# A three-layer max-aggregation graph network: blocks of two kinds interleaved, byte stores moved to ScalarE's queue, and the cut of long edge lists changed

## The chip, the cores and the metric

One core of one Trainium2 chip runs the whole kernel. The metric is the device time of one execution in microseconds; the time before is the median of 3 runs. TensorE (PE) multiplies, VectorE (DVE) takes maxima, ScalarE (ACT) builds one-hot matrices, GpSimd (POOL) issues indirect gathers, SyncE (SP) issues nearly all other transfers from one in-order queue.

## The reference

```python
N, E, D, H = 6250, 200000, 128, 256          # nodes, edges (sorted by dst), widths
h = relu(layernorm(x))
for Wl, bl, Wr in three layers (128->256, 256->256, 256->128):
    agg = segment_max(h[src], dst, N)        # 0 where a node has no edge
    h = leaky_relu(agg @ Wl + bl + h @ Wr, 0.01)
out = x + h
```

`dst` is drawn as 6250 u², so the first nodes have hundreds of edges and the last some ten.

## The kernel before

**Tiles and blocks.** The nodes are cut into 50 tiles of 127. Two neighbouring tiles of sources form a group `g`, 25 in all, taken from 24 down to 0. For every group and every tile of destinations, the kernel holds per destination node at most one source in the group (or two, one for each tile `s` of the pair). A one-hot matrix (`hot`) times the two tiles of features (`pair_sb`) puts that source's features into PSUM (`pg`, three buffers), and DVE takes the maximum with the running result `acc`. Features are split in two parts so that the products are exact, hence two products for each output.

**Units.** A destination tile is *narrow* (one source for a pair: both `s` add up in one `pg`, one maximum for a step) or *wide* (one source for each `s`: two `pg` and two maxima for a step, with the same products). There are four sets, numbered `k`: 0 is 24 narrow tiles, 1 is 8 *virtual* units (1024 rows of at most 64 edges that stand for the 381 nodes with the most edges; each is a wide unit and a narrow one called `x`), 2 is 19 wide tiles, 3 is 4 narrow tiles. A block `(layer, k, g)` is cut into steps of 8 products: in the layers 1 and 2 (the second and third) a block has 6, 4, 5 and 1 steps for k = 0 to 3, so that a layer has 400 steps; layer 0, with half the width, has 225.

**Edges that don't fit.** Edges left over (a second source in the same group) stand in lists, one list for each set, sorted by length: `CAPS[k][q]` is how many entries the q-th column of 128 rows may have. Each entry is one indirect gather of 128 feature rows on POOL (`g`, L997, with a small `pace_t` memset behind it); DVE folds them (L1012, L1017), and SP stores the result to `best` (L1021). If some list is longer than its cap, a slow general path computes everything anew.

**Nodes.** When a set's products and lists are done, `Node` runs for each of its tiles: gather from `best` (L1041), transposes, maximum `mz`, the two linear products (L1070, L1072), and for layers 0 and 1 the stores that feed the next layer (`table`, `across`, `pair`). For the virtual set, `Joined` first merges and scans the 1024 rows and sends them to `joined`; then the three tiles with the longest lists have their nodes.

**What sets the order.** One loop over steps writes all engines' programs. It takes the steps in the order of `steps`: within a layer, all blocks of k = 0, then 1, 2, 3. Lists, nodes and setup work are planned at step numbers (`agenda`), counted from `ends_at[layer, k]`, the step at which a set's blocks end: 150, 250, 375 and 400 of a layer's 400 before. `load_pair` runs two blocks ahead (three buffers), `load_idx` three ahead.

**One-hots.** In layer 0, `one_hot` reads the stored source numbers (`idx_sb`), writes `away` (bytes, three buffers; L924) and from it `hot` (six buffers; L931). `away` is also stored to `far` in DRAM (450 stores, L926), so that the layers 1 and 2 can make `hot` from it directly. SP's queue carries these stores, each one issued when the next one-hot is made (`unsent`). ACT must wait for a store to land before it writes that `away` buffer again.

Of the kernel before, what the change touches and what calls it, by code (L numbers as in the profile page):

```python
# [32 lines left out]
F32 = mybir.dt.float32  # L33
# [6 lines left out]
OP = mybir.AluOpType  # L40
AX = mybir.AxisListType

P = 128
# [6 lines left out]
CUT = 64  # L50
# [3 lines left out]
VT, NV = 3, 8  # L54
CAPS = (
# [4 lines left out]
)  # L60
# [8 lines left out]
def kernel(ctx: ExitStack, tc: tile.TileContext, x, src, dst,  # L69
                    Wl1, bl1, Wr1, Wl2, bl2, Wr2, Wl3, bl3, Wr3, out):  # L70
    nc = tc.nc
# [5 lines left out]
    NG = NT // 2  # L77
# [15 lines left out]
    GROUPS = (  # L93
        [("n", i) for i in range(24)],
        [("w", NW + v) for v in range(NV)],
        [("w", i) for i in range(NW)],
        [("n", i) for i in range(24, NN)],
    )
# [20 lines left out]
    psum = ctx.enter_context(tc.tile_pool(name="psum", bufs=1, space=bass.MemoryType.PSUM))  # L119
# [28 lines left out]
    far = [dram.tile([P, NG, DW[k]], U8, name=f"far{k}") for k in range(len(GROUPS))]  # L148
# [12 lines left out]
    first = setup.enter_context(tc.tile_pool(name="first", bufs=1))  # L161
# [181 lines left out]
    at_n = edge.tile([P, NT], F32, name="at_n")  # L343
    at_i = edge.tile([P, NT], I32, name="at_i")
    count_n = edge.tile([P, NT], F32, name="count_n")
# [30 lines left out]
    rem = edge.tile([P, NV], F32, name="rem")  # L376
# [261 lines left out]
    def virtual():  # L638

        nrow_i = first.tile([P, VT], I32, name="nrow_i")  # L640
        nc.vector.tensor_scalar(nrow_i, count_n[:, :VT], float(CUT - 1), None, op0=OP.add)
        nc.vector.tensor_scalar(nrow_i, nrow_i, CUT.bit_length() - 1, None, op0=OP.arith_shift_right)
        nrow = first.tile([P, VT], F32, name="nrow")
        nc.vector.tensor_copy(nrow, nrow_i)
        pre = first.tile([P, VT], F32, name="pre")
        nc.vector.memset(pre, 0.0)
        for c in range(1, VT):
            nc.vector.tensor_add(pre[:, c : c + 1], pre[:, c - 1 : c], nrow[:, c - 1 : c])
        v_p = psum.tile([P, VT], F32, tag="z", name="v_p")
        nc.tensor.matmul(v_p, before, nrow, start=True, stop=False)  # L650
        nc.tensor.matmul(v_p, ones, pre, start=False, stop=True)
        iota_r = first.tile([P, NV * P], F32, tag="xs0", name="iota_r")
        for v in range(NV):
            nc.vector.tensor_scalar(iota_r[:, v * P : (v + 1) * P], iota_f, float(v * P), None, op0=OP.add)
        vs = first.tile([P, VT], F32, name="vs")
        nc.vector.tensor_copy(vs, v_p)
        ve = first.tile([P, VT], F32, name="ve")
        nc.vector.tensor_add(ve, vs, nrow)
        ab = first.tile([P, VT, 2], F32, name="ab")
        nc.vector.scalar_tensor_tensor(ab[:, :, 0], vs, -float(CUT), at_n[:, :VT], op0=OP.mult, op1=OP.add)  # L660
        nc.vector.scalar_tensor_tensor(ab[:, :, 1], vs, float(CUT), count_n[:, :VT], op0=OP.mult, op1=OP.add)
        of_p = psum.tile([P, NV, 2], F32, tag="tr", name="of_p")
        sels = []
        for c in range(VT):
            under = first.tile([P, NV * P], F32, tag="xs1", name="under")
            nc.vector.tensor_scalar(under, iota_r, ve[:, c : c + 1], None, op0=OP.is_lt)
            sel = first.tile([P, NV * P], F32, tag=f"xs{2 + c}", name="sel")
            nc.vector.scalar_tensor_tensor(sel, iota_r, vs[:, c : c + 1], under, op0=OP.is_ge, op1=OP.mult)
            sels.append(sel)
        for v in range(NV):  # L670
            for c in range(VT):
                nc.tensor.matmul(
                    of_p[:, v, :], sels[c][:, v * P : (v + 1) * P], ab[:, c, :], start=(c == 0), stop=(c == VT - 1)
                )
        has = first.tile([P, VT], F32, name="has_v")
        nc.vector.tensor_scalar(has, nrow, 1.0, None, op0=OP.min)
        starts = first.tile([P, VT, NV * P], BF16, tag="pr0", name="starts", bufs=2)
        for c in range(VT):
            nc.vector.tensor_scalar(
                starts[:, c, :], iota_r, vs[:, c : c + 1], has[:, c : c + 1], op0=OP.is_equal, op1=OP.mult  # L680
            )
        st_p = psum.tile([P, 2, 512], F32, tag="pg", name="st_p", bufs=3)
        for h in range(2):
            for c in range(VT):
                nc.tensor.matmul(
                    st_p[:, h, :], ones_h, starts[:, c, h * 512 : (h + 1) * 512], start=(c == 0), stop=(c == VT - 1)
                )
        by_row = first.tile([P, NV], F32, name="by_row")
        nc.vector.tensor_scalar(by_row, iota_f[:, :NV], float(P), part_f, op0=OP.mult, op1=OP.add)
        nc.vector.tensor_scalar(by_row, by_row, float(CUT), None, op0=OP.mult)  # L690
        nc.vector.tensor_tensor(pos_i, of_p[:, :, 0], by_row, op=OP.add)
        nc.vector.tensor_tensor(rem, of_p[:, :, 1], by_row, op=OP.subtract)
        nc.vector.tensor_scalar(
            mask_v, st_p.rearrange("p h c -> p (h c)"), -2.0, 1.0, op0=OP.mult, op1=OP.add
        )
        nc.vector.tensor_scalar(mask_v, mask_v, BIG, None, op0=OP.mult)
        last = first.tile([P, VT], F32, name="last")
        nc.vector.scalar_tensor_tensor(last, ve, -float(NV * P + 1), has, op0=OP.add, op1=OP.mult)
        nc.vector.tensor_scalar(last, last, 0.0, float(NV * P), op0=OP.min, op1=OP.add)
        nc.vector.tensor_copy(last_i, last)  # L700
        beyond = first.tile([P, VT], F32, name="beyond")
        nc.vector.tensor_scalar(beyond, ve, float(NV * P), None, op0=OP.is_gt)
        nc.vector.reduce_sum(over[:, 4:5], beyond, axis=AX.X)
# [168 lines left out]
    def chunks(layer, k):  # L872

        n = 8 if widths[layer] == P else 4
        units = PLANES[k]
        for w in "wnx":
            us = [i for i, u in enumerate(units) if u[0] == w]
            for i0 in range(0, len(us), n):
                part = us[i0 : i0 + n]
                yield part[0] - (NV if w == "x" else 0), len(part) * P, part[0], units[part[0]][1] if w == "w" else None  # L880
# [31 lines left out]
                yield us[i0], len(us[i0 : i0 + HOT // P]) * P, len(GROUPS[k]) if w == "w" else 0  # L912

    hots, live, done_with = {}, [0], [0, 0]
    unsent = []

    def one_hot(layer, k, g, c, w, odd, s):

        t, of = idx_q[layer, k, g]
        put = 2 * c * P + s * w  # L920
        if layer == 0:
            at = of + (c + (odd if s else 0) + (NV if PLANES[k][c] in EXTRA else 0)) * P
            away = work.tile([P, HOT], U8, tag="away", name="away", bufs=3)[:, :w]
            nc.scalar.activation(away, t[:, at : at + w], AF.Abs, bias=near[:, s : s + 1], scale=1.0)  # L924
            if unsent:
                nc.sync.dma_start(*unsent.pop())  # L926
            unsent.append((far[k][:, g, put : put + w], away))
        else:
            away = t[:, of + put : of + put + w]
        hot = work.tile([P, HOT], F32R, tag="hot", name="hot", bufs=HOTS)  # L930
        nc.scalar.activation(hot[:, :w], away, AF.Relu, bias=1.0, scale=-1.0)  # L931
        hots[layer, k, g, c, s] = hot
        live[0] += 1

# [200 lines left out]


    steps, begins, ends_at = [], [], {}
    for layer in range(3):
        begins.append(len(steps))
        for k in range(len(GROUPS)):  # L1140
            for g in range(NG - 1, -1, -1):
                steps += [(layer, k, g, c) for c in chunks(layer, k)]
            ends_at[layer, k] = len(steps)
    begins.append(len(steps))
    agenda = {}
# [70 lines left out]
    for layer in range(3):  # L1216
# [45 lines left out]
        for k in range(NL):  # L1262
            t0 = max(ends_at[layer, k], done_at[k] + gap) + 1
# [22 lines left out]
            if k == NL - 1:  # L1286
                t0 = max(end, done_at[k] + 1) + 1
# [29 lines left out]
    def load_until(n):  # L1317
        while loaded[0] < min(n, len(blocks)):
            load_idx(*blocks[loaded[0]])
            loaded[0] += 1  # L1320

    def make_hots(t, most):

        while jobs_h and most and live[0] < HOTS and jobs_h[0][0] <= t + LOOK:
            most -= 1
            _, b, job = jobs_h.pop(0)
            if job[0] and unsent:
                nc.sync.dma_start(*unsent.pop())
            load_until(b + 1 + AHEAD)
            one_hot(*job)  # L1330

# [20 lines left out]
    for t in range(max(max(agenda)[0] + 1, len(steps) + 1)):  # L1352
# [10 lines left out]
        if t < len(steps):  # L1363
            st = steps[t]
            layer, k, g, _ = st
# [313 lines left out]
```

## Time and profile before

| | |
|---|---|
| Median of 3 runs | 3476.97 us (3474.94 to 3482.45) |
| The profiled execution | 3516.21 us, span 3514.4 us |
| PE busy | 2570.8 us (73%) |
| DVE busy | 2686.4 us (76%) |
| ACT busy | 1894.1 us (54%) |
| POOL busy | 2444.0 us (70%) |
| DMA | 639.71 MB, mean 182 GB/s |

No engine is busy throughout, and each stage has its own limit, so the shares of the whole span say little; the stages have to be read one by one. Counted along the products, setup ends at about 266 us, layer 0 runs to 1440, layer 1 to 2490, layer 2 to 3489.

### The profile page before, as it was taken

What the parts mean: (1) busy time and instruction counts of PE and PEld (TensorE: products, weight loads), DVE (VectorE), ACT (ScalarE), POOL (GpSimd) and SP (SyncE); (2) the same over time, 40 slices, a digit from 0 to 9 for tenths busy, and PEclk for the clock granted to TensorE, in tenths of its full rate; (3) what the DMA queues carried; (4) which work ended last, traced back from release to release, by engine and by line L of the source; (5) the groups of instructions that cost most, each with busy time, mean ns of one, the idle gap of its engine ahead of it and who ended that gap; (6) DMA issues with size and microseconds to landing.
All of it is one profiled execution on the core that took longest, in us unless ns stands there. A gap on an engine that the chain in (4) does not pass through costs nothing. (4 is left out here: it accounts for less than half of the span.)

```text
span 3514.4 us, 39180 instructions
## 1 busy us (share of the span) xinstructions
PE 2570.8 (73%) x9920; PEld 1816.2 (52%) x9920; DVE 2686.4 (76%) x4152; ACT 1894.1 (54%) x2762; POOL 2444.0 (70%) x3460
## 2 busy tenths in 40 slices
PE   1025642457766677799988978788999999787776
PEld 1013321234434444588766655556788776555555
DVE  6567799796555664588867989996688889899974
ACT  5106962687998997555434434343555534333432
POOL 5588742747667876388856867767388888777673
PEclk9976875579887777899999989999999999999998
DMA  9114421447866558676777755459776777655475
GB/s 293 44 42 124 142 87 42 110 121 212 232 177 187 181 168 244 214 211 217 215 219 225 211 163 169 158 162 306 255 214 226 225 222 204 177 173 168 147 221 172
DMA packets 347946, 639.71 MB, mean 182 GB/s; under 512 B 67830, under 2 KB 215939, under 8 KB 347073
## 3 DMA queue, kind: packets, MB, share of 16 engines
q1 hardware_dynamic: 268161, 438.67, 38.2%
q0 software_dynamic: 79488, 198.26, 22.5%
q8 instruction: 83, 1.36, 0.2%
q14 instruction: 150, 1.23, 0.1%
q10 hardware_dynamic: 64, 0.20, 0.0%
HBM read 494.73 MB, written 142.15 MB: 181 GB/s over the span
## 5 line engine op out<-in xcount | busy, mean ns | idle before, releaser
L948 PE MATMUL pg<-hot,pair_sb 128*128 128x512 f32 (+1 forms) x8000 | 2257.3, 429 | 536.5 <-ACT hot L931 249.6
L948 PEld LDWEIGHTS pg<-hot,pair_sb 128*128 128x128 f32 x8000 | 1540.3, 204 | 1124.2 <-ACT hot L931 442.3
L997 POOL DMA_INDIRECT g<-table,let x1530 | 1543.9, 1009 | 765.6 <-ACT let L986 320.7
L965 DVE TENSOR_TENSOR acc<-acc,pg 128x1024 f32<-128x1024 f32 (+3 forms) x1439 | 1647.2, 1168 | 484.1 <-PE pg L948 338.3
L931 ACT ACTIVATE hot<-idx_sb 128x1024 fp32r<-128x1024 uint8 (+2 forms) x900 | 827.0, 948 | 732.8 <-PE pg L948 463.1
L924 ACT ACTIVATE away<-idx_sb,near 128x1024 uint8<-128x1024 uint8 (+2 forms) x450 | 464.4, 1032 | 210.1 <-DMA far<-away 178.0
L1001 POOL MEMSET pace_t<- 128x300 bf16 x1530 | 560.3, 366 | 1.0
L931 ACT ACTIVATE hot<-away 128x1024 fp32r<-128x1024 uint8 (+2 forms) x450 | 427.7, 951 | 14.3
L1041 POOL DMA_INDIRECT agg<-best,end_i x141 | 138.6, 983 | 134.5 <-PE aT_p L1057 46.5
L1074 ACT COPY s<-z_p 127x256 f32<-127x256 f32 (+1 forms) x150 | 49.9, 333 | 329.4 <-PE z_p L1072 182.1
L1012 DVE TENSOR_TENSOR g<-g 128x1024 f32<-128x1024 f32 (+6 forms) x218 | 219.6, 1007 | 1.6 <-DMA g<-table,let 1.5
L1017 DVE TENSOR_TENSOR g<-g 128x512 f32<-128x512 f32 (+3 forms) x351 | 172.9, 493 | 10.2
L1070 PE MATMUL z_p<-wr,hT_in 128*128 128x256 f32 (+1 forms) x500 | 137.4, 392 | 7.1 <-DMA hT_in<-across 7.1
L1072 PE MATMUL z_p<-wl,mz 128*128 128x256 f32 (+1 forms) x500 | 122.0, 361 | 9.0 <-DVE mz L1063 7.6
L986 ACT ACTIVATE let<-ell 128x4 int32<-128x4 int16 (+3 forms) x444 | 81.5, 190 | 84.7 <-issue 84.7
L1063 DVE TENSOR_TENSOR mz<-acc,aT_p 128x256 f32<-128x256 f32 (+1 forms) x141 | 52.5, 372 | 83.5 <-PE aT_p L1057 62.0
L1072 PEld LDWEIGHTS z_p<-wl,mz 128*128 128x128 f32 x500 | 89.4, 204 | 21.7 <-DVE mz L1063 8.9
L1070 PEld LDWEIGHTS z_p<-wr,hT_in 128*128 128x128 f32 x500 | 80.0, 201 | 29.4 <-DMA hT_in<-across 7.6
L352 POOL DMA_INDIRECT win_d<-in_dst_dram,win_i x50 | 53.2, 1063 | 45.5 <-ACT rstd L305 14.7
L857 DVE TENSOR_TENSOR pr<-h,pr 128x256 fp32r<-128x256 f32 x100 | 42.4, 424 | 49.0 <-ACT pr L852 37.3
L622 POOL DMA_INDIRECT picks<-picked,to_i x55 | 57.2, 1039 | 30.0 <-DVE rank_f L599 14.1
L849 ACT COPY hT<-hT_p 128x254 f32<-128x254 f32 x100 | 36.3, 363 | 69.9 <-PE hT_p L847 61.1
(268 smaller groups left out, 1195.1 us busy)
## 6 DMA issues: line engine op xcount, KB each, us to landing
pair_sb<-pair SPq DMA_DIRECT2D x200, 512.0 KB
far<-away SPq DMA_DIRECT2D x350, 128.0 KB
idx_sb<-far SPq DMA_DIRECT2D x50, 768.0 KB
idx_sb<-far SPq DMA_DIRECT2D x50, 608.0 KB
pair_sb<-pair SPq DMA_DIRECT2D x100, 256.0 KB
pair<-pr SPq DMA_DIRECT2D x100, 256.0 KB
idx_sb<-far SPq DMA_DIRECT2D x50, 512.0 KB
g<-table,let POOLq DMA_INDIRECT x1530
```

Source lines behind the costliest of these rows:

```text
L924: nc.scalar.activation(away, t[:, at : at + w], AF.Abs, bias=near[:, s : s + 1], scale=1.0)
L931: nc.scalar.activation(hot[:, :w], away, AF.Relu, bias=1.0, scale=-1.0)
L948: nc.tensor.matmul(to, pr[:, s, i, kk * P : (kk + 1) * P], hot[:, o : o + bw], start=((alone or s == 0) and i == 0), stop=((alone or s == ...
L965: nc.vector.tensor_max(to, to, of)
L986: nc.scalar.activation(let[:, :n], ell[self.k][:, q, j : j + n], AF.Identity, scale=1.0)
L997: nc.gpsimd.indirect_dma_start(out=self.tiles[q, b][:, i, :], out_offset=None, in_=tables[self.layer], in_offset=bass.IndirectOffsetOnAxis ...
L1001: nc.gpsimd.memset(pace_t, 0.0)
L1012: nc.vector.tensor_max(base[:, : i + 1, :], base[:, : i + 1, :], g[:, : i + 1, :])
L1017: nc.vector.tensor_max(base[:, :h, :], base[:, :h, :], base[:, w - h : w, :])
L1041: nc.gpsimd.indirect_dma_start(out=self.agg[:, : self.F], out_offset=None, in_=of, in_offset=bass.IndirectOffsetOnAxis(ap=at, axis=0),)
L1070: nc.tensor.matmul(z_p, self.hT[:, i, :], wr[layer][:, i, :], start=False, stop=False)
L1072: nc.tensor.matmul(z_p, self.m[:, i, :], wl[layer][:, i, :], start=False, stop=(i == K - 1))
```

## The change

Three things are changed together. **The order of blocks**: in the layers 1 and 2 each set gets a stretch of the layer (`SPANS`), its 25 blocks are placed evenly in it, and all blocks are sorted by place. Wide blocks (k = 2) are spread over the first 0.9 and so stand between the narrow ones (over the first 0.45) and the virtual ones (0.45 to 0.78); k = 3 comes last. Layer 0 keeps its order. **The stores** of `away` go out from ACT's queue, directly behind the `hot` made of it. **Virtual rows**: a node's edges are split evenly over its rows (at most 64 each) where before each row but the last had 64. The row count stays; `CAPS[1]` goes from 86 entries to 70.

```diff
-    (22, 15, 14, 12, 11, 9, 2, 1),
+    (21, 12, 10, 9, 7, 5, 4, 2),
...
-        ab = first.tile([P, VT, 2], F32, name="ab")
-        nc.vector.scalar_tensor_tensor(ab[:, :, 0], vs, -float(CUT), at_n[:, :VT], op0=OP.mult, op1=OP.add)
-        nc.vector.scalar_tensor_tensor(ab[:, :, 1], vs, float(CUT), count_n[:, :VT], op0=OP.mult, op1=OP.add)
+        has = first.tile([P, VT], F32, name="has_v")
+        nc.vector.tensor_scalar(has, nrow, 1.0, None, op0=OP.max)
+        each = first.tile([P, VT], F32, name="each")
+        nc.vector.reciprocal(each, has)
+        nc.vector.scalar_tensor_tensor(each, each, 1.0, count_n[:, :VT], op0=OP.mult, op1=OP.mult)
...
+        nc.vector.tensor_scalar(each, each, float(CUT), None, op0=OP.min)
+        ab = first.tile([P, VT, 3], F32, name="ab")
...
+        nc.vector.tensor_tensor(rem, of_p[:, :, 2], rem, op=OP.min)
...
-            if unsent:
-                nc.sync.dma_start(*unsent.pop())
-            unsent.append((far[k][:, g, put : put + w], away))
         else:
             away = t[:, of + put : of + put + w]
         hot = work.tile([P, HOT], F32R, tag="hot", name="hot", bufs=HOTS)
         nc.scalar.activation(hot[:, :w], away, AF.Relu, bias=1.0, scale=-1.0)
+        if layer == 0:
+            nc.scalar.dma_start(far[k][:, g, put : put + w], away)
...
+    SPANS = ((0, 0.45), (0.45, 0.78), (0, 0.9), (0.9, 1))
+
+    def place(layer, k, g):
+        t0, t1 = SPANS[k] if layer else (k, k + 1)
+        return t0 + (t1 - t0) * (NG - g - 0.5) / NG
+
     for layer in range(3):
         begins.append(len(steps))
-        for k in range(len(GROUPS)):
-            for g in range(NG - 1, -1, -1):
-                steps += [(layer, k, g, c) for c in chunks(layer, k)]
+        for _, k, g in sorted((place(layer, k, g), k, g) for k in range(len(GROUPS)) for g in range(NG)):
+            steps += [(layer, k, g, c) for c in chunks(layer, k)]
             ends_at[layer, k] = len(steps)
```

In the layers 1 and 2 the sets now end at the steps 210, 355, 375 and 400; 60 wide steps lie among the first 210, 45 among the next 145, 20 stand alone.

SP's queue in layer 0, in the blocks of k = 0, before (`far` are the byte stores, `best` the list results, `pair_sb` and `idx_sb` what the next blocks need):

```order
L926 DMA far_155<-away 128x1024
L1021 DMA best_0_140<-g 128x128
L926 DMA far_155<-away 128x1024
L903 DMA pair_sb<-pair_4_82 128x512
L926 DMA far_155<-away 128x1024 x3
L1021 DMA best_0_140<-g 128x128
L926 DMA far_155<-away 128x1024
L892 DMA idx_sb<-idx_151 128x3072
```

The same place of SP's queue now:

```order
L906 DMA idx_sb<-idx_151 128x3072
L1033 DMA best_0_140<-g 128x128
L917 DMA pair_sb<-pair_4_82 128x512
L1033 DMA best_0_140<-g 128x128
L906 DMA idx_sb<-idx_151 128x3072
```

And ACT's program there now, with what each row waits for (`DMAHW` are eight counters that the transfers of both queues use in turn):

```order
L937 ACTIVATE away<-idx_sb,near 128x1024
L941 ACTIVATE hot<-away 128x1024 [waits Activation_49]
L943 DMA far_155<-away 128x1024 [waits DMAHW0_49]
L937 ACTIVATE away<-idx_sb,near 128x1024
L941 ACTIVATE hot<-away 128x1024 [waits Activation_49]
L943 DMA far_155<-away 128x1024 [waits DMAHW1_49]
L937 ACTIVATE away<-idx_sb,near 128x1024 [waits DMAHW7_49]
```

A store no longer stands behind a list result; it stands in ACT's program, where it can wait for an earlier transfer's counter.

DVE near the start of layer 1, before (`acc_1568` is the running result of the narrow tiles, L965 the maxima, L1012 and L1017 the folds of gathers):

```order
L965 TENSOR_TENSOR acc_1568<-acc_1568,pg 128x2x512 x3
L1012 TENSOR_TENSOR g<-g 128x1024
L965 TENSOR_TENSOR acc_1568<-acc_1568,pg 128x2x512 x3
L1012 TENSOR_TENSOR g<-g 128x768
L1017 TENSOR_TENSOR g<-g 128x512
L1017 TENSOR_TENSOR g<-g 128x256
L965 TENSOR_TENSOR acc_1568<-acc_1568,pg 128x2x512 x7
```

And now (`acc_1582` narrow, `acc_1583` wide):

```order
L977 TENSOR_TENSOR acc_1582<-acc_1582,pg 128x2x512 x3
L977 TENSOR_TENSOR acc_1583<-acc_1583,pg 128x2x512 x3
L1024 TENSOR_TENSOR g<-g 128x1024
L977 TENSOR_TENSOR acc_1583<-acc_1583,pg 128x2x512 x5
L977 TENSOR_TENSOR acc_1583<-acc_1583,pg 128x2x384 x2
L1024 TENSOR_TENSOR g<-g 128x1024
L977 TENSOR_TENSOR acc_1582<-acc_1582,pg 128x2x512 x2
```

A wide block's ten maxima now come after every twelve narrow ones.

More of the change, by code (lines that the diff above doesn't have):

```diff
@@ L658, in virtual @@
         nc.vector.tensor_add(ve, vs, nrow)
-        ab = first.tile([P, VT, 2], F32, name="ab")
-        nc.vector.scalar_tensor_tensor(ab[:, :, 0], vs, -float(CUT), at_n[:, :VT], op0=OP.mult, op1=OP.add)
-        nc.vector.scalar_tensor_tensor(ab[:, :, 1], vs, float(CUT), count_n[:, :VT], op0=OP.mult, op1=OP.add)
-        of_p = psum.tile([P, NV, 2], F32, tag="tr", name="of_p")
+        has = first.tile([P, VT], F32, name="has_v")
[3 more added lines that the diff above has]
+        nc.vector.scalar_tensor_tensor(each, each, 1.0, count_n[:, :VT], op0=OP.mult, op1=OP.mult)
+        nc.vector.tensor_copy(nrow_i, each)
+        nc.vector.tensor_copy(each, nrow_i)
+        short = first.tile([P, VT], F32, name="short")
+        nc.vector.tensor_mul(short, each, nrow)
+        nc.vector.tensor_tensor(short, short, count_n[:, :VT], op=OP.is_lt)
+        nc.vector.tensor_add(each, each, short)
+        nc.vector.tensor_scalar(each, each, float(CUT), None, op0=OP.min)
+        ab = first.tile([P, VT, 3], F32, name="ab")
+        nc.vector.tensor_mul(ab[:, :, 2], vs, each)
+        nc.vector.tensor_sub(ab[:, :, 0], at_n[:, :VT], ab[:, :, 2])
+        nc.vector.tensor_add(ab[:, :, 1], count_n[:, :VT], ab[:, :, 2])
+        nc.vector.tensor_copy(ab[:, :, 2], each)
+        of_p = psum.tile([P, NV, 3], F32, tag="tr", name="of_p")
         sels = []
@@ L674, in virtual @@
                 )
-        has = first.tile([P, VT], F32, name="has_v")
         nc.vector.tensor_scalar(has, nrow, 1.0, None, op0=OP.min)
@@ L689, in virtual @@
         nc.vector.tensor_scalar(by_row, iota_f[:, :NV], float(P), part_f, op0=OP.mult, op1=OP.add)
-        nc.vector.tensor_scalar(by_row, by_row, float(CUT), None, op0=OP.mult)
+        nc.vector.tensor_tensor(by_row, of_p[:, :, 2], by_row, op=OP.mult)
         nc.vector.tensor_tensor(pos_i, of_p[:, :, 0], by_row, op=OP.add)
         nc.vector.tensor_tensor(rem, of_p[:, :, 1], by_row, op=OP.subtract)
+        nc.vector.tensor_tensor(rem, of_p[:, :, 2], rem, op=OP.min)
         nc.vector.tensor_scalar(
@@ L914 @@
     hots, live, done_with = {}, [0], [0, 0]
-    unsent = []
     def one_hot(layer, k, g, c, w, odd, s):
@@ L1326, in make_hots @@
             _, b, job = jobs_h.pop(0)
-            if job[0] and unsent:
-                nc.sync.dma_start(*unsent.pop())
             load_until(b + 1 + AHEAD)
```

## The prediction

> **What bounds the kernel now.** I read the busy shares first. No engine is near full, so the whole span decides nothing:
>
> ```profile
> PE 2570.8 (73%) x9920; PEld 1816.2 (52%) x9920; DVE 2686.4 (76%) x4152; ACT 1894.1 (54%) x2762; POOL 2444.0 (70%) x3460
> ```
>
> Then the table by stretches. Its borders come from counting the products L948 in order (8 to a step in the layers 1 and 2), so that a stretch holds one set of blocks. The columns are length, then busy time of PE, weight loads, DVE, ACT and POOL, then granted clock, DMA share, GB/s.
>
> ```profile
> 266.00:771.00 505.00, 250.43 (x674) 149.09 (x675) 415.42 (x1052) 329.92 (x361) 296.76 (x435) 0.68 0.37 102
> 771.00:1032.00 261.00, 181.23 (x603) 111.37 (x602) 150.50 (x274) 233.74 (x303) 175.15 (x251) 0.86 0.73 205
> 1032.00:1323.00 291.00, 194.47 (x540) 118.42 (x540) 182.77 (x232) 271.27 (x364) 225.27 (x330) 0.78 0.60 177
> 1323.00:1440.00 117.00, 80.23 (x254) 45.36 (x255) 46.20 (x105) 81.72 (x166) 61.59 (x81) 0.76 0.82 241
> 1440.00:1500.00 60.00, 57.79 (x243) 45.30 (x243) 38.38 (x42) 34.19 (x51) 27.87 (x40) 0.95 0.69 206
> 1500.00:1724.00 224.00, 224.00 (x990) 185.55 (x989) 185.93 (x190) 127.93 (x169) 198.97 (x291) 1.00 0.69 216
> 1724.00:1910.00 186.00, 163.28 (x701) 120.31 (x699) 133.42 (x170) 72.64 (x136) 117.98 (x163) 0.96 0.74 219
> 1910.00:2020.00 110.00, 102.18 (x417) 74.73 (x418) 103.56 (x96) 55.31 (x74) 91.48 (x130) 1.00 0.79 218
> 2110.00:2383.00 273.00, 220.56 (x799) 144.23 (x797) 263.07 (x260) 107.23 (x163) 199.44 (x293) 0.95 0.52 163
> 2383.00:2490.00 107.00, 99.40 (x446) 75.12 (x447) 64.11 (x99) 45.31 (x107) 62.29 (x83) 0.97 0.98 327
> 2775.00:2913.00 138.00, 130.94 (x655) 99.73 (x654) 124.78 (x167) 54.65 (x91) 114.38 (x156) 1.00 0.75 228
> 2913.00:3021.00 108.00, 100.11 (x410) 73.10 (x410) 104.07 (x98) 53.27 (x68) 90.98 (x131) 1.00 0.77 214
> ```
>
> Layer 0 is the first four rows: DVE carries the first (415 of 505, setup work among the maxima), ACT the second and third (271 of 291). In layer 1, narrow blocks (1500 to 1724) keep PE full while DVE has 38 us to spare, and wide blocks (2110 to 2383) keep DVE full (263 of 273). Between them lie the virtual blocks, with the narrow tiles' nodes in the first half. The last, k = 3 with nodes, has the DMA at 0.98. Layer 2 has the same shape.
>
> **Narrow and wide steps.** The groups of maxima in the two stretches, and who waits in the wide one:
>
> ```profile
> L965 DVE TENSOR_TENSOR acc<-acc,pg 128x1024 f32<-128x1024 f32 x124 | 149.2, 1218 | 35.8 <-PE pg L948 30.1 <-issue 4.4 <-DVE acc L965 0.6
> L965 DVE TENSOR_TENSOR acc<-acc,pg 128x1024 f32<-128x1024 f32 (+1 forms) x200 | 224.7, 1164 | 8.8 <-PE pg L948 1.0 <-issue 0.5
> PE pg L948 <- DVE acc L965: 31.7, 51, 2.7
> ```
>
> 124 maxima are 124 narrow steps: 224/124 = 1.806 us each, all PE; DVE needs 185.93/124 = 1.50. 200 maxima are 100 wide steps: 2.73 each; DVE needs 2.63, PE 1.806. DVE waits for PE in the one and PE for DVE in the other.
>
> **The first 210 steps of the layers 1 and 2** now hold 150 narrow and 60 wide steps. In 1440 to 1500, 25 steps with the previous layer's last nodes, PE is full (57.79 of 60) and DVE is at 38.38; if ten of these steps are wide, DVE has 38.4 + 10 × 1.22 = 51, still below 60. The other 185 steps (135 narrow, 50 wide) need 185 × 1.806 = 334 us of PE and 135 × 1.50 + 50 × 2.63 = 334 of DVE. Before, the same 210 steps took 60 + 125 × 1.806 + 60 × 2.73 = 450. After it is 60 + 334 = 394 if both overlap fully, and 60 + 135 × 1.806 + 50 × 2.73 = 440 if each block keeps its own pace. A wide block leaves DVE at most three `pg` behind, 3 × 1.22 = 3.7 us, which the twelve narrow steps behind it absorb (12 × 0.3 = 3.6); twelve wide blocks give 44 at most. DVE lost 10 of 273 where it always had work, and here both engines are full, so I take 36 us saved in each layer, **−72**; ends −112 and −20.
>
> **The virtual stretch**, 100 virtual and 45 wide steps, has less to give. Its second half already runs at DVE's pace (103.56 of 110; 2.2 us a step). Only the first half, with the nodes, has DVE idle: 133.42 of 186. Of its 48 steps 15 become wide; DVE rises by 15 × (2.63 − 2.07) = 8 us, inside the idle time, and 15 virtual steps more are done behind it at 2.2 instead of 15 wide at 2.73. That is 8 us, and with the two steps that no longer lie in the node half some 10 for layer 1. In layer 2 DVE has 124.78 of 138 and takes only part: 5. **−15**; ends −30 and +10 (nodes that wait longer for DVE).
>
> **The joined rows** now come behind step 355, not 250. Their transposes and scans stood among wide steps and still do; but the three nodes behind them move from there, where PE had room, to the border of the k = 3 stretch, where PE has 99.40 of 107 and the DMA is at 0.98. The large products of one node, from the node stretch (24 nodes):
>
> ```profile
> L1070 PE MATMUL z_p<-wr,hT_in 128*128 128x256 f32 x96 | 30.4, 444 | 0.0
> L1072 PE MATMUL z_p<-wl,mz 128*128 128x256 f32 x96 | 26.8, 405 | 0.0
> ```
>
> 57.2/24 = 2.4 us, so 3 × 2.4 = 7 us, of which some lies in the last wide steps: 5 for each layer, **+10**; ends 0 and +30, if the chain of gather, scan and store, too, is waited for in the 20 steps that are left.
>
> **The byte stores.** The waits of layer 0, first stretch, then the far stores' waits in the next three stretches:
>
> ```profile
> ACT away L924 <- DMA far<-away: 140.0, 15, 27.1
> DVE acc L965 <- PE pg L948: 39.9, 15, 16.3
> DVE acc L965 <- issue: 20.9, 5, 15.9
> SPq L1021 <- DVE g L1017: 169.8, 17, 32.1
> SPq L632 <- DMA picks<-picked,to_i: 21.0, 1, 21.0
> ACT away L924 <- DMA far<-away: 9.5, 11, 1.6
> ACT away L924 <- DMA far<-away: 11.2, 11, 2.8
> ACT away L924 <- DMA far<-away: 17.2, 12, 3.6
> ```
>
> ACT stands still for a store that is not issued: SP waits up to 32 us for DVE's folds (L1021), once 21 us for a list (L632), and the store is behind. One such place:
>
> ```profile
> 346.45 0.32 SPq L632 DMA_DIRECT2D ell<-picks  x1
> 346.86 0.38 SPq L926 DMA_DIRECT2D far<-away  x1
> 348.76 1.15 ACT L924 ACTIVATE away<-idx_sb,near 128x1024 uint8<-128x1024 uint8 x1 [16.64 <-DMA far<-away]
> 353.17 1.22 DVE L965 TENSOR_TENSOR acc<-acc,pg 128x1024 f32<-128x1024 f32 x1 [16.31 <-PE pg L948]
> ```
>
> ACT's stall becomes DVE's a few us later. Most of the 140 us are hidden behind DVE's setup work; what can come back is DVE's waiting, 39.9 + 20.9 = 61 us. With its own queue ACT can run ahead until the six `hot` are full, three steps. I take 45 (the two long stalls, 32, and half of the rest); ends 0 and 61. Pair and index loads stay behind SP's waits, but two and three blocks ahead. In the second and third stretch ACT is the bound, so nearly all of 9.5 and 11.2 counts: 17. In the fourth the DMA is at 0.82: 5 of 17.2. **−67**; ends 0 and −99.
>
> The cost is the issue, which now holds ACT's sequencer:
>
> ```profile
> L926 SPq DMA_DIRECT2D far<-away x449: 13/382/1403, 264.7 to 1424.6; - x150
> L931 ACT ACTIVATE hot<-away x450: 522/1057/1062, 264.7 to 1425.1; 128x1024 fp32r<-128x1024 uint8 x109, 128x384 fp32r<-128x384 uint8 x25, 128x512 fp32r<-128x512 uint8 x16
> ```
>
> 0.38 us stands behind a `hot` of 1.06 (0.52 for the narrowest) that is already running, so I take 0. If it is exposed it is 450 × 0.38 = 171. SP loses the same 171 us, but it mostly waits, so nothing follows.
>
> The Trainium skill speaks against this part: "DMA: Bandwidth & Descriptors", section "Issuing engines are not separate DMA queues", says that transfers started by several engines run on the same 16 DMA engines and only the issue time is saved. By that rule alone the term would be 0 (the rival below). The trace disagrees so far as the time lost here lies ahead of the issue, in SP's waits of 169.8 us.
>
> **The rest.** 16 gathers fewer in each layer. POOL isn't the bound anywhere, but DVE's folds of them are; in 1500 to 1724:
>
> ```profile
> L1012 DVE TENSOR_TENSOR g<-g 128x1024 f32<-128x1024 f32 (+3 forms) x22 | 19.6, 892 | 1.0 <-DMA g<-table,let 0.9
> L1017 DVE TENSOR_TENSOR g<-g 128x256 f32<-128x256 f32 (+1 forms) x44 | 23.6, 535 | 1.2
> L997 POOL DMA_INDIRECT g<-table,let x146 | 148.0, 1014 | 26.6 <-issue 21.9 <-ACT hot L931 2.7 <-DVE acc L965 0.7
> ```
>
> 43.2/146 = 0.3 us a gather: 5 in each of the layers 1 and 2, of which 3 where DVE bounds: **−6**; ends 0 and −15. The even split adds twelve instructions on 128x3 to DVE's setup, like
>
> ```profile
> L658 DVE TENSOR_TENSOR ve<-vs,nrow x1: 163/163/163, 191.2 to 191.2; 128x3 f32<-128x3 f32 x1
> ```
>
> 12 × 0.16 = 2 us ahead of the first one-hot: **+2**; ends 0 and +3. Counted from the reference's inputs, the longest lists of the eight columns are then 19, 12, 10, 9, 7, 5, 4, 2, within the new caps, so the general path isn't run.
>
> **Sum**: −72 − 15 + 10 − 67 − 6 + 2 = −148 us against the profiled 3516.21. That execution stands 1.1% above the median; scaled, 146 us off 3476.97 is **3331 us**.
>
> **Rivals.**
> - *Blocks keep their own pace* (three `pg` absorb little): the first 210 steps save 20, not 72, so 52 less, **3383**. For it: narrow steps leave DVE only 0.3 us each. Against: 12 × 0.3 is what a wide block leaves.
> - *The stores gain nothing*, because SP's loads stand behind the same waits, or by the skill's rule that only issue time is saved: 67 less, **3398**. For it: `idx_sb` and `pair_sb` are still in that queue. With the first rival together, **3449**.
> - *Better*: full overlap, all of DVE's and ACT's waits recovered (−112, −99): 72 more, **3259**. The 0.96 of the wide stretch speaks against both engines being full.
> - *Slower*: ACT's program now contains the waits. Each store waits for a counter that an earlier transfer used, of SP too, and takes 0.38 us of issue; if that is exposed, everything behind it on ACT (next `hot`, `let` for POOL, node copies) waits, and PE for `hot`. 171 us lost and the 67 not gained: 3331 + 67 + 171 = **3569**. It decides from 81/450 = 0.18 us exposed per store. Against it: the running `hot` is longer than the issue.
>
> **Chances.** Forecast 0.40, own pace 0.17, no gain from stores 0.14, both 0.04, better 0.12, slower 0.09, losses that just cancel 0.04. So faster 0.87, within 0.2% (7 us, about what three runs here can tell apart) 0.04, slower 0.09. The range 3245 to 3430 holds all but 0.17; the likeliest case's own is 3300 to 3365.
>
> **What would show it.** Right: in the first 210 steps of layer 1 DVE and PE both above 0.9, in about 414 us; the wait of `away` for `far` below 40 us in all and DVE's waits for `pg` in layer 0's first stretch below 25; no gap of ACT behind a store; the k = 3 stretch 5 us longer. Wrong: DVE still idle in narrow blocks and PE in wide ones; ACT's one-hots more than 2.2 us apart in layer 0's third stretch; a joined chain that leaves PE empty behind step 355.

## The result, and the profile after

The changed kernel takes 3419.17 us (median of 4 runs, 3414.62 to 3420.28); the kernel before, run beside it, 3479.71. The ratio is 0.9824, 95% interval [0.9806, 0.9842]: 61 us faster, 55 to 68 by the interval, where the forecast was 146. The time lies in the range of the prediction (3245 to 3430), near its upper end and outside its likeliest case's own (3300 to 3365). The profiled execution took 3414.62 us, span 3412.8.

The busy shares hardly moved:

```profile
PE 2530.9 (74%) x9919; PEld 1800.4 (53%) x9920; DVE 2676.0 (78%) x4160; ACT 1889.6 (55%) x2750; POOL 2385.0 (70%) x3364
```

The stretches, with borders again from counting the products. The first four rows are layer 0 (k = 0 to 3); then layer 1 in five pieces: steps 0 to 25, 25 to 210 (narrow and wide blocks), 210 to 355 (virtual and wide blocks, nodes), 355 to 375, 375 to 400; then the second and third of these pieces for layer 2. Columns as in the prediction.

```profile
239.00:720.00 481.00, 232.63 (x675) 146.89 (x676) 418.42 (x1056) 328.90 (x362) 295.74 (x432) 0.70 0.39 108
720.00:978.00 258.00, 179.99 (x604) 109.83 (x604) 152.37 (x277) 233.25 (x301) 166.79 (x241) 0.87 0.71 207
978.00:1258.00 280.00, 191.84 (x540) 114.07 (x538) 178.65 (x226) 270.13 (x362) 216.47 (x319) 0.79 0.60 181
1258.00:1365.00 107.00, 76.81 (x253) 40.80 (x254) 45.75 (x106) 81.81 (x165) 61.51 (x81) 0.82 0.87 263
1365.00:1423.00 58.00, 54.60 (x232) 41.10 (x231) 42.45 (x47) 32.25 (x51) 28.93 (x42) 0.98 0.66 206
1423.00:1800.00 377.00, 352.84 (x1480) 271.46 (x1481) 336.44 (x334) 195.84 (x264) 312.14 (x451) 1.00 0.64 198
1800.00:2218.00 418.00, 362.07 (x1475) 262.57 (x1474) 354.06 (x376) 175.52 (x279) 283.12 (x401) 0.96 0.62 198
2218.00:2292.00 74.00, 51.79 (x217) 38.63 (x215) 61.83 (x70) 21.14 (x40) 51.24 (x72) 0.93 0.54 164
2292.00:2404.00 112.00, 102.86 (x463) 77.39 (x461) 64.53 (x102) 48.92 (x118) 63.49 (x83) 0.95 0.96 324
2464.00:2844.00 380.00, 355.85 (x1482) 273.71 (x1481) 336.29 (x335) 195.49 (x263) 311.32 (x451) 0.99 0.63 196
2844.00:3211.00 367.00, 328.59 (x1424) 241.04 (x1423) 347.13 (x376) 156.71 (x230) 284.55 (x401) 0.98 0.64 199
```

Against the terms of the sum ("before" for a mixed stretch is what the same steps took apart: narrow blocks 285, a wide step 2.73):

| Term | forecast | by the two profiles |
|---|---|---|
| First 210 steps, both layers | −72 | 449 → 435.6 and 449 → 439.8: −23 |
| Virtual stretch | −15 | 418.2 → 417.7 and 369.5 → 367.3: −3 |
| Joined rows (steps 355 to 400) | +10 | 183.0 → 186.1 and 179.7 → 180.6: +4 |
| Byte stores (layer 0) | −67 | 1173 → 1125: −48 |
| Gathers and split, −6 + 2 | −4 | inside the other rows |
| Sum | −148 | −70 (the runs: −61) |

Setup up to the first product, 239 us here and 266 in the profile before, is no gain: with the setup of before it took 238 us and 235 us in two runs below. Over all executions shown here it lay between 235 and 285.

The mixed rows, at first reading, look as forecast: in 1423 to 1800 PE shows 352.84 of 377, DVE 336.44. But PE's 1480 products cost 238 ns of busy time each where the narrow stretch before had 226 (224.00 for 990), so 0.94 is not 0.94 of its pace. At 226 ns the 1480 products are 334 us, and 43 us are lost: 24 as PE's idle time, the rest as longer products. What PE waited for there, most of it for DVE and nothing for `pair_sb`, and DVE for PE:

```profile
PE pg L960 <- DVE acc L977: 15.0, 29, 2.0
PE pg L960 <- ACT hot L941: 5.6, 13, 1.3
DVE acc L977 <- PE pg L960: 33.3, 67, 0.6
```

**Where they are lost** is seen at one wide block and its neighbours (1591.39 to 1604.07 is the wide block, before and after it six narrow steps), in a table by windows:

```profile
1580.51:1591.39 10.88, 10.88 (x49) 9.01 (x48) 8.60 (x9) 6.18 (x10) 9.58 (x15) 1.00 0.64 204
1591.39:1604.07 12.68, 10.32 (x42) 6.77 (x40) 12.10 (x13) 6.05 (x8) 9.73 (x14) 1.00 0.62 197
1604.07:1615.05 10.98, 10.98 (x49) 9.08 (x49) 10.03 (x12) 5.67 (x8) 8.24 (x12) 1.00 0.63 213
```

and in the timelines of PE and of DVE over the same place (start, length, instruction, in brackets the idle time ahead of it and what ended it):

```profile
1579.83 15.38 PE L960 MATMUL pg<-hot,pair_sb 128*128 128x512 f32 x67
1596.74 4.69 PE L960 MATMUL pg<-hot,pair_sb 128*128 128x512 f32 x16 [1.53 <-DVE acc L977]
1601.66 0.94 PE L960 MATMUL pg<-hot,pair_sb 128*128 128x384 f32 x4 [0.22 <-DVE acc L977]
```

```profile
1589.78 1.22 DVE L977 TENSOR_TENSOR acc<-acc,pg 128x1024 f32<-128x1024 f32 x1 [0.43 <-PE pg L960]
1591.59 2.35 DVE L977 TENSOR_TENSOR acc<-acc,pg 128x1024 f32<-128x1024 f32 x2 [0.59 <-PE pg L960]
1593.86 0.42 DVE L1024 TENSOR_TENSOR g<-g 128x256 f32<-128x256 f32 x1
1594.32 1.15 DVE L1029 TENSOR_TENSOR g<-g 128x512 f32<-128x512 f32 x2
1595.38 10.51 DVE L977 TENSOR_TENSOR acc<-acc,pg 128x1024 f32<-128x1024 f32 x9
```

PE runs at its own pace to the end of the second wide step, then waits for DVE; DVE, which still waited 0.43 and 0.59 us at the block's entry, is busy without a gap from 1591.59 to 1605.9 (two folds, 1.6 us, stand among its maxima). The six narrow steps before take 10.88, PE's pace exactly, with DVE idle for 2.28. So only the block's first step or two are absorbed. Counted over all blocks of 1423 to 1800, the steps last (a narrow block's first step, not listed, takes 1.91):

| Step | us, mean | DVE's last maximum ends behind PE's last product, us |
|---|---|---|
| narrow, second and later | 1.81 | 1.4 to 1.7 |
| wide, first in its block | 2.03 | 2.5 |
| wide, second | 2.65 | 3.1 |
| wide, third to fifth | 2.71 to 2.74 | 2.5 to 3.0 |

A wide block leaves DVE some 1.5 us further behind, not the 3.7 of the forecast. The likely reason is that of the three `pg` one holds a result that DVE reads and one is being filled; the number of buffers was not varied in any run.

**Layer 0, first stretch**, the waits that answer to those shown before:

```profile
ACT hot L941 <- PE pg L960: 80.7, 5, 31.3
ACT let L998 <- DMA g<-table,let: 19.3, 1, 19.3
ACT away L937 <- DMA far<-away: 5.3, 2, 3.0
DVE acc L977 <- PE pg L960: 32.0, 14, 13.7
SPq L1033 <- DVE g L1029: 210.8, 21, 35.2
SPq L632 <- DMA picks<-picked,to_i: 52.2, 2, 28.9
```

140.0 us of waiting for the store became 5.3, and ACT now waits for free `hot` buffers, ahead of PE. But one long stall is left. ACT's, SP's and DVE's timelines there:

```profile
308.13 1.06 ACT L941 ACTIVATE hot<-away 128x1024 fp32r<-128x1024 uint8 x1
327.94 0.33 ACTq L943 DMA_DIRECT2D far<-away  x1
328.44 0.20 ACT L998 ACTIVATE let<-ell 128x4 int32<-128x4 int16 x1 [19.26 <-DMA g<-table,let]
```

```profile
324.58 0.32 SPq L632 DMA_DIRECT2D ell<-picks  x1
```

```profile
335.07 1.22 DVE L977 TENSOR_TENSOR acc<-acc,pg 128x1024 f32<-128x1024 f32 x1 [13.66 <-PE pg L960]
```

The store behind the `hot` of 308.13 goes out only at 327.94, 19 us late, and ACT stands for it. The row names a gather; what comes just ahead is SP's load of a list, itself up to 28.9 us late. In the program the transfers of SP and ACT take one of eight completion counters in turn, and a transfer waits until the one before it on its counter has landed. For this store that one is a load of `pair_sb`, which SP issues at 324.99, directly behind the late list. The run with the stores alone, below, names that load in its trace, and the run with later list loads takes the wait away.

### The profile page after: what moved, and what is told of

Its sections match the earlier page's. It is cut to its first block, busy times and chain, and to the rows that moved or that the text cites. A ratio compares the mean times of both kernels' runs of the same rounds, so it can differ in the third digit from the quotient of the medians.

```text
span 3412.8 us, 38645 instructions
## 1 busy us (share of the span) xinstructions
PE 2530.9 (74%) x9919; PEld 1800.4 (53%) x9920; DVE 2676.0 (78%) x4160; ACT 1889.6 (55%) x2750; POOL 2385.0 (70%) x3364
## 5 line engine op out<-in xcount | busy, mean ns | idle before, releaser
L960 PE MATMUL pg<-hot,pair_sb 128*128 128x512 f32 (+1 forms) x8000 | 2218.5, 424 | 464.7 <-ACT hot L941 234.2
L1009 POOL DMA_INDIRECT g<-table,let x1482 | 1500.0, 1012 | 731.3 <-ACT let L998 314.7
L1013 POOL MEMSET pace_t<- 128x300 bf16 x1482 | 542.1, 366 | 0.9
L1024 DVE TENSOR_TENSOR g<-g 128x1024 f32<-128x1024 f32 (+6 forms) x208 | 205.7, 989 | 9.2 <-DMA g<-table,let 9.1
L1029 DVE TENSOR_TENSOR g<-g 128x256 f32<-128x256 f32 (+3 forms) x357 | 175.4, 491 | 10.2
```

The lines of the kernel that those rows point to most:

```text
L960: nc.tensor.matmul(to, pr[:, s, i, kk * P : (kk + 1) * P], hot[:, o : o + bw], start=((alone or s == 0) and i == 0), stop=((alone or s == ...
L1009: nc.gpsimd.indirect_dma_start(out=self.tiles[q, b][:, i, :], out_offset=None, in_=tables[self.layer], in_offset=bass.IndirectOffsetOnAxis ...
L1013: nc.gpsimd.memset(pace_t, 0.0)
L1024: nc.vector.tensor_max(base[:, : i + 1, :], base[:, : i + 1, :], g[:, : i + 1, :])
L1029: nc.vector.tensor_max(base[:, :h, :], base[:, :h, :], base[:, w - h : w, :])
```

## The experiments

Theory O: the wide blocks' term failed because only about one `pg` of backlog fits, so whole blocks keep DVE's pace and single wide steps would not. Theory S: what the stores' term lacks is the stall through SP's list loads. The rivals stand with each run. Each run was timed in five rounds beside the kernel before.

**The three parts alone.** From the kernel before, the order of blocks:

```diff
+    SPANS = ((0, 0.45), (0.45, 0.78), (0, 0.9), (0.9, 1))
...
+        for _, k, g in sorted((place(layer, k, g), k, g) for k in range(len(GROUPS)) for g in range(NG)):
...
```

> The kernel before with the new order of blocks alone (no moved stores, no even split). Theory O (a wide block leaves DVE only about one result buffer behind, since at its border the other two are being filled and read): in the changed kernel's trace a wide block lasts 12.82 us in its five steps where five wide steps alone take 13.65, so 0.85 us for each of 12 to 14 blocks in the first 210 steps of layers 1 and 2; about -20 us in all with the virtual stretch and the joined rows, 3450 to 3462. Rival F (the forecast: engines overlap fully, and the stores' part ate the gain): -72 - 15 + 10 = -77, about 3400. Rival 0 (no effect): 3477.

Measured: 3455.47 us, ratio 0.9911 [0.9898, 0.9925], so −31 us [−36, −26]. More than theory O's −20, less than half of −77. Its first 210 steps took 439 and 437 us, as in the changed kernel: own pace, −22. The rest of the gain lies in the virtual stretch (steps 210 to 355: 411.1 and 362.4, −7 in each layer).

The stores:

```diff
-            if unsent:
-                nc.sync.dma_start(*unsent.pop())
-            unsent.append((far[k][:, g, put : put + w], away))
...
+        if layer == 0:
+            nc.scalar.dma_start(far[k][:, g, put : put + w], away)
...
```

> The kernel before with the byte stores on ACT's queue alone. Theory O: layer 0 takes 1125 us in the changed kernel's trace where it took 1173, so -35 to -50 us, 3427 to 3442; the wait of away for far below 40 us. Forecast: -67, 3410. Rival (only issue time is saved, so nothing): 3477. Also read here: whether setup up to the first product takes 266 us as in the profiled execution of before, or some 240.

Measured: 3439.4 us, 0.9865 [0.985, 0.988], −47 us [−52, −42], and not the forecast's 67. In its one profile layer 0 takes 1140 us where it took 1173, so −33, less than the −48 of the changed kernel, and the layers 1 and 2, which the edit does not touch, are 4 and 6 shorter, as single profiles can be. The long stall is here too, and its row says what ended it, a transfer of SP:

```profile
331.78 1.15 ACT L923 ACTIVATE away<-idx_sb,near 128x1024 uint8<-128x1024 uint8 x1 [20.87 <-DMA pair_sb<-pair]
```

The Trainium skill's rule weighed in the prediction ("DMA: Bandwidth & Descriptors", section "Issuing engines are not separate DMA queues") gave 0 for this part by itself; the run disagrees, because what was lost stood ahead of the issue, in the queue's order.

The even split:

```diff
-    (22, 15, 14, 12, 11, 9, 2, 1),
+    (21, 12, 10, 9, 7, 5, 4, 2),
...
```

> The kernel before with the even split of virtual rows and the smaller caps alone: 16 gathers fewer in each layer, twelve small DVE instructions more in setup. Forecast: -6 + 2 = -4 us; rival: the gathers are hidden everywhere, 0 to +2. Under either 3469 to 3479, and setup up to the first product as in e2 or 2 us more.

Measured: 3480.95 us, 0.999 [0.9979, 1.0002], −3.5 us [−7, +1]: the forecast of −4 fits, and so does nothing.

The product of the three ratios is 0.977, −81 us, where the changed kernel has −61. That is taken up below.

**Single steps in place of blocks.** The changed kernel, with each step placed by itself, free lists for the three `pair_sb` and four `idx_sb` buffers, and wide one-hots made 512 wide in the layers 1 and 2:

```diff
-        for _, k, g in sorted((place(layer, k, g), k, g) for k in range(len(GROUPS)) for g in range(NG)):
-            steps += [(layer, k, g, c) for c in chunks(layer, k)]
+        for k in range(len(GROUPS)):
+            cs = list(chunks(layer, k))
+            for g in range(NG):
+                placed += [(place(layer, k, g, (j + 0.5) / len(cs)), k, g, j, c) for j, c in enumerate(cs)]
+        for _, k, g, _, c in sorted(placed, key=lambda q: q[:4]):
+            steps.append((layer, k, g, c))
...
-            load_until(b + 1 + AHEAD)
             one_hot(*job)
+            jobs_left[b] -= 1
+            if not jobs_left[b]:
+                free_idx.append(idx_of.pop(b))
+                next_idx()
...
```

> The changed kernel with single steps in place of whole blocks interleaved in the first 0.9 of layers 1 and 2 (a wide step, then two or three narrow or virtual steps), and the one-hots of wide steps in the layers 1 and 2 made 512 wide instead of 1024, so that six buffers serve two blocks at once. Theory O (only about one result buffer, 1.2 us, of DVE's backlog fits): a single wide step leaves DVE 2.63 - 1.81 = 0.82 us behind, which fits, and the next two or three narrow steps give it back (0.3 each); so most of 60 x 0.82 us in each of two layers is saved, less the 10 that whole blocks save already: -40 to -60 us against the changed kernel, first 210 steps of layer 1 about 410 us instead of 436. Rival E (DVE and PE are both as good as full once folds and nodes are counted, so the grain does not matter): within 7 us of the changed kernel. Rival H (one-hots in smaller pieces and shared buffers come late, PE waits for ACT): 10 to 60 us slower than the changed kernel, with PE's waits for hot in the hundreds of times.

Measured: 3399.12 us, 0.9749 [0.9736, 0.9763]. The changed kernel was at 0.9824 in its own comparison, so some −26 us, half of theory O's. First 210 steps: 430 and 437 us, hardly less than 436 and 440, which by itself would speak for rival E. But the waits of PE in steps 25 to 210 of layer 1 name something new:

```profile
PE pg L966 <- DMA pair_sb<-pair: 15.0, 8, 4.4
PE pg L966 <- DVE acc L983: 9.4, 15, 1.4
```

A wide step now lasts 2.07 us in place of 2.7, and the gain goes to pairs that come late: a narrow and a wide block are open at once, a third buffer is all there is to load ahead, and two blocks can begin one behind the other. A fourth buffer, in the space that is free from layer 1 on, tells the two theories apart:

```diff
             for i in (1, 2):
                 load_layer(i, later, later)
+            free_pair.append(later.tile([P, 4 * H], F32R, name="pair_sb3"))
+            next_pair()
```

> The kernel with single steps interleaved, with a fourth buffer for pair_sb in the layers 1 and 2. In its run with three buffers PE waited in steps 25 to 210 of layer 1 for pair_sb 15.0 us (8 times, up to 4.4), and lone wide steps lasted 2.07 us instead of the 2.7 of a wide block's later steps. Theory O (lone wide steps fit into one result buffer; what ate the gain is pairs that come late): the 15 us go, steps 25 to 210 about 358 us instead of 373.5, -25 to -35 us against three buffers, some -50 against the changed kernel. Rival E (PE and DVE are near full anyway, another wait takes its place): at most -10 against three buffers.

Measured: 3402.24 us on a slower chip (the kernel before: 3522.82), 0.9658 [0.9632, 0.9685]; the changed kernel, run with it, 0.982. So −55 us against whole blocks and, by the ratios, −32 against three buffers: both as theory O says. The same kernel once more, with the next runs:

> Single steps interleaved, four pair buffers, with the moved stores and the even split, once more, as the yardstick for the kernels run with it: ratio to the kernel before 0.963 to 0.969, as measured.

Measured: 3355.88 us, 0.9631 [0.9615, 0.9648]. Its row for steps 25 to 210 of layer 1, and all that PE waited for there:

```profile
1432.30:1788.70 356.40, 344.09 (x1482) 273.69 (x1481) 334.06 (x335) 203.25 (x307) 304.78 (x454) 1.00 0.69 211
```

```profile
PE pg L966 <- DVE acc L983: 10.1, 13, 1.4
PE pg L966 <- ACT let L1004: 0.8, 1, 0.8
PE pg L966 <- ACT hot L947: 0.7, 1, 0.7
```

356.40 in place of 377, with the same 1.5 us of backlog to use and DVE's work unchanged (334.06 beside 336.44). The first 210 steps are 412 and 414 us; the forecast had 414 for this stretch. Not all of the gain need come from the grain: PE's waits for `hot` fell from 5.6 to 0.7 us, so up to 5 of the 21 us may belong to the narrower one-hots, and whole blocks were not run with them. The fourth buffer alone can't have helped whole blocks, as PE never waited for `pair_sb` there. The place of the example above is now one run of PE without a wait, 117 products in 27.49 us (235 ns each, so still not PE's best pace):

```profile
1578.62 27.49 PE L966 MATMUL pg<-hot,pair_sb 128*128 128x512 f32 x117
```

Mixing alone, at this grain, from the kernel before (no moved stores, no split):

> The kernel before with single steps interleaved and a fourth pair buffer, without moved stores and without the even split: what the mixing alone is worth at this grain. The forecast's own terms for mixing (first 210 steps -72, virtual stretch -15, joined rows +10) sum to -77. Theory O: with the grain of a step these hold, -65 to -80 us, ratio 0.977 to 0.981. Rival (the gain of the yardstick over whole blocks, some 55 us, needs the moved stores too): -35 to -55, ratio 0.984 to 0.990.

Measured: 3400.09 us, 0.976 [0.9742, 0.9778], −84 us [−90, −77], a little more than theory O had. The sum of the forecast's three terms for mixing, −77, holds for single steps; by the traces it is made of −66 for the first 210 steps, −12 for the virtual stretch and −4 (not +10) for the rest. For whole blocks the same mixing gave −31.

**The stall of the stores.** The changed kernel, with the loads of the later lists put behind source-number work that stood after them:

```diff
-        chores.append((0, load))
+        return lambda: chores.append((0, load))
...
-    late_rows(1)
+    load_1 = late_rows(1)
     late_lookups(LISTS[1], 0)
+    load_1()
...
```

> The changed kernel with the three loads of later lists (ell, from picks) put some steps later in SP's program, behind source-number work on DVE that came after them, so that SP no longer waits there for the lists to land (52.2 us in layer 0's first stretch, once 28.9). Theory S (the one long gap of DVE, 13.7 us at 335 us, comes from a byte store that waits for a completion counter held by a transfer behind that wait of SP): the gap and ACT's 19.3 us wait ahead of it go, first stretch of layer 0 about 467 us instead of 481, -14 us in all. Rival: another SP wait (for DVE's folds, 35 us) holds the same counters, or DVE's setup work fills the time, so 0 to -4 us.

Measured, on the slower chip: 3443.76 us, 0.9779 [0.9747, 0.9811], beside 0.982 [0.9794, 0.9845] for the changed kernel. That could not settle it: the intervals overlap, the first stretch is 472 us beside 474, and in that chip's profile of the changed kernel the long stall was not there (DVE's longest wait for `pg` 4.5 us). It comes and goes with the timing: on that chip the kernel without the split lacks it too and the one with four pairs has it (14.9), on the other chip all four kernels with moved stores and the old list loads have it (13.6 to 14.9). So the same edit went onto the kernel with single steps and four pairs:

> The yardstick with the loads of the later lists put some steps later. With whole blocks this gave a ratio of 0.9779 [0.9747, 0.9811] beside 0.982 [0.9794, 0.9845], while the first stretch of layer 0 was only 2 us shorter by the profiles. If the gain was real: -8 to -14 us again; if it was scatter of setup: within 4 us.

Measured: 3338.79 us, 0.9567 [0.9547, 0.9586], beside 3355.88, 0.9631, without it: −17 us, no overlap. The waits of DVE and ACT in the first stretch of layer 0, first without the edit,

```profile
DVE acc L983 <- PE pg L966: 32.8, 14, 13.6
ACT let L1004 <- DMA g<-table,let: 18.7, 1, 18.7
SPq L632 <- DMA picks<-picked,to_i: 51.7, 2, 28.4
```

and with it (SP has no wait for `picks` left):

```profile
DVE acc L983 <- PE pg L966: 14.9, 12, 2.9
SPq L1039 <- DVE g L1035: 231.8, 24, 35.2
```

The windows of the two stretches:

```profile
238.00:720.00 482.00, 230.56 (x674) 145.14 (x675) 418.29 (x1053) 328.33 (x360) 293.85 (x434) 0.70 0.40 107
```

```profile
237.00:701.00 464.00, 225.82 (x673) 142.21 (x674) 418.66 (x1053) 327.87 (x361) 296.67 (x434) 0.72 0.41 111
```

18 us shorter with the same DVE work. SP's wait for a list was what held ACT's store (theory S); by the program and the trace with the stores alone it did so through the counter that the store shares with SP's pair load. SP's waits for folds, 231.8 us, are still there and stop no store for long. The counter itself was not tried apart: no run gave the stores counters of their own.

**Do the parts add?** The changed kernel once more, and with the split undone:

> The changed kernel once more, as the yardstick for the other kernels run with it. The three parts alone gave ratios of 0.9911, 0.9865 and 0.999 to the kernel before, whose product is 0.977 (-81 us); the changed kernel gave 0.9824 (-61). If the parts simply add, this run gives 0.977; if they get in each other's way, 0.982 again.

Measured: 3457.53 us, 0.982 [0.9794, 0.9845]: the same ratio as before; the product, 0.977 [0.974, 0.979] by the intervals of its three factors, is just outside, so the parts do not simply add.

> The changed kernel with the even split and the smaller caps undone (order of blocks and stores as in the changed kernel). In the layers 1 and 2 the steps 150 to 210 and 300 to 330 took 2 to 5 us longer in the changed kernel than with the new order alone, 15.5 us in all, although it has 16 gathers fewer in a layer. Theory: the smaller caps shift the folds of lists against the wide blocks, so undoing them makes the changed kernel 5 to 15 us faster. Rival (the parts add; noise of single profiles): 3 to 6 us slower than the changed kernel.

Measured: 3459.29 us, 0.9811 [0.9788, 0.9833], no difference to 0.982. In the traces the layers 1 and 2 are 8 us shorter each without the split (means of two runs without, three with; the 12 and 14 of the expectation below do not come out), steps 150 to 210 and 300 to 330 by 2 to 5 each; the times don't show it. And at the grain of single steps:

> The same without the even split (old caps, 16 gathers more in a layer). With whole blocks the split cost 12 and 14 us in the layers 1 and 2 by the traces and nothing by the times. Theory L (the loss is in which steps the lists' folds fall, wide blocks above all): with single steps no row of wide steps is left for a fold to fall into, so undoing the split costs the 3 to 6 us of the forecast. Rival: the split costs there too, so undoing it gains 5 to 15 us.

Measured: 3371.57 us, 0.9681 [0.9664, 0.9698], beside 3355.88: without the split 16 us slower, more than the 3 to 6 of theory L, and the rival is out. Between the two traces steps 25 to 210 differ by 2 and 5 us, the rest is in pieces of 1 to 4. So on one chip the split is worth −4 with the old order and −16 with single steps, and on the slower chip 0 with whole blocks. That its worth depends on the order is shown by the first two; where the 16 gathers meet the wide steps was only read from the stretches.

The stores don't add to the new order either. At the grain of single steps they are worth 28 us without the split (3400.09 to 3371.57), not 47; with whole blocks the order and the stores without the split are at 0.9811 where their product is 0.9777, 12 us short, though on two chips. Why is open, and with it most of the 20 us by which the parts don't add: one kernel on the two chips already differs by 0.3% (0.9658 and 0.9631).

## Why the prediction was right or wrong

- **What bounds the kernel**: right. Narrow blocks are PE's, wide ones DVE's. DVE's sum of 334 us is what it then worked (334.06 to 336.44); the stretch itself came down to 356 us at best, and of the 22 us above both sums only 12 are waits of PE that the trace names.
- **The first 210 steps, −72**: wrong for this change; this is the largest part of the miss, 49 of 78 us by the two profiles. The step that failed: "A wide block leaves DVE at most three `pg` behind, 3 × 1.22 = 3.7 us, which the twelve narrow steps behind it absorb". The narrow steps could absorb it, but it never arises: 1.5 us fit, a wide block runs at 2.7 us a step from its second step on, and saves some 0.85 us; 24 such blocks are 20 of the 23 us measured. The rival "own pace" had −20. The value came out for single steps with a fourth buffer, 412 and 414 us instead of 449, but this is another kernel, and the 36 us were chosen between ends of 10 and 56, so that it fits to the microsecond is luck.
- **The virtual stretch, −15**: −14 with the new order alone, −3 in the changed kernel. The mechanism (nodes' idle time of DVE filled) was not tested, and where the 11 us went stays open: without the split the changed kernel's trace has 407.3 and 362.5 for these steps, so −18, but the times show no such gain.
- **The joined rows, +10**: +4 by the stages, so about half of the size.
- **The stores, −67**: direction and mechanism right, the size too high. It counted "the two long stalls, 32" as gone; one of the two stayed, since a moved store can still wait for SP. Layer 0's first stretch gave 25 us where the forecast had 45, the other three 23 where it had 22. With later list loads (single steps, four pairs) the first stretch is 464 us, 41 less than before, but the other three are only 12 less, so layer 0 gives 52 there: the forecast of the first stretch nearly holds, the 67 were never reached. The cost of the issue, 0, was right: at 306.00 the `hot` and its store's issue (0.33 us) start together, and the next `away` follows the `hot` without a gap.
- **"Slower"** named this mechanism (a store that waits for a counter that a transfer of SP used) but priced it on every store; it struck once in layer 0's first stretch, for 19 us.
- **Gathers and split, −4**: −3.5 alone.
- **What would show it**: the wait of `away` for `far` is 12.4 us in all of layer 0 (below 40, right); DVE's waits for `pg` in its first stretch are 32.0 (below 25, wrong, by the one stall); PE and DVE in the first 210 steps are at 0.94 and 0.87, in 436 us, not 414 (wrong); the k = 3 stretch is 5.3 us longer in layer 1 and the same in layer 2 (half right).

With both repairs the kernel takes 3338.79 us beside 3483.01, −144 us, near what the forecast expected of the change by itself. The sum agrees by chance, its parts don't: from run to run, mixing gives 83 us (forecast 77), the stores with later lists 28 + 17 (67) and the split 16 (4).

## What to carry to other kernels

Two engines that alternate as the bound overlap only as far as the buffers between them let one run ahead: count the backlog that really fits (here 1.5 us of three buffers worth 3.7), and alternate in units that are smaller than it (here −84 us instead of −31 for the same mixing). Finer alternation opens more inputs at once, so look for the load that comes late next (here 15 us of waits for `pair_sb`). Moving a transfer to another engine's queue freed it here from that queue's order (−47 us), but not from the counters that the two queues share; planning away a wait in the old queue gave another 17.

## What was not expected of the hardware

- PE's busy time per product is not constant in these profiles: 226 ns in a PE-bound stretch, 238 in the mixed one, where DVE holds PE up, at a granted clock of 1.00 in both. The ends of products are modelled in the profile and their records overlap, so this need not be a slower PE. A busy share of PE near 0.94 can hide 11% of lost time (377 us for 334 of products).
- Executions differ most in setup: up to the first product 235 to 240 us in eight of the twelve experiments, 270 to 285 in the four on one chip, where the kernel before is 36 to 40 us slower too (3522.82 beside 3487.06 and 3483.01). A difference of tens of us in a single profile is to be looked for there first.
